# Layer 0 of a four-layer graph network: adj turned by transposing transfers instead of TensorE in six of sixteen batches

## The chip, the core and the metric

The kernel runs on one NeuronCore of a Trainium2 chip, as one launch. The metric is device time in microseconds, the median of three runs. The engines are TensorE (PE, with its weight loads PEld), VectorE (DVE), ScalarE (ACT), GpSimd (POOL) and SyncE (SP). SP and POOL issue the transfers; a transfer issued by SP is on the hardware queue, one issued by POOL on the software queue. Both share the core's 16 DMA engines.

## The reference

Input is `x` of 16 x 1024 x 128 float32 and a 0/1 matrix `adj` of 16 x 1024 x 1024 int32. Four layers follow each other, each adding to `x`. Only layer 0 is touched by the change:

```python
adjT = jnp.transpose(adj.astype(jnp.float32), (0, 2, 1))
w = _masked_row_softmax(adjT)
region = jnp.matmul(w, features)
region = jnp.matmul(region, kernel_1) + bias_1
region = _batch_norm(region, gamma_1, beta_1)
people = jnp.matmul(jnp.transpose(w, (0, 2, 1)), region)
people = jnp.matmul(people, kernel_2) + bias_2
people = _batch_norm(people, gamma_2, beta_2)
```

`features` is relu of the layer norm of `x`. As adj holds 0 and 1, a row of the softmax is the row of adjT over its sum, so two products with adj are needed: one with adjT and one with adj itself. The batch norms take their statistics over all batches; layers 1 to 3 (attention per batch) start when they are known.

## The kernel before, in words

**Rows.** For each of 16 batches, `first_layer` loads the 1024 rows of adj as eight tiles `a` of 128 x 1024, cast to fp8 by the transfer (L372, issued by POOL, 18 places of `a`, so a little over two batches). `load_x` (L366) fetches x.

**Features.** DVE and POOL make the layer norm and split it in two float16 halves in `hv` (`stats`, `aggregate`, `power`, `centre`, `upper`, `lower`; L382 to L401).

**Turning adj.** For the second product adj must lie turned in `at`. In `turn` (L418) TensorE transposes the rows, two fp8 at a time as one float16 word: a step is eight transposes into one PSUM bank, four steps to a batch. `square` (L426) then takes every other byte of the bank by ACT, squares it (0 and 1 stay) and sums each row into `sums`: two squares to a bank, eight to a batch. `share` (L434 to L437, DVE) makes the reciprocals `rc` of the row sums.

**First product.** `product` (L459) is eight steps of eight matmuls, each step into a PSUM bank of its own. `low` (L463, ACT) scales the low half by `rc`, `join` (L467, DVE) adds the halves into `r`; after both the bank is free. `high` (L471, POOL) and `rest` (L474, DVE) make `rv`. `spread` (L352) adds `r` to a gram matrix.

**Second product.** `product2` (L499) is eight steps of eight matmuls with `at`; `low2` (L503, ACT) and `join2` (L506, DVE) empty the bank into `g`, `spread2` (L352) adds to the second gram matrix, and two `turn2` steps (L533) with `save` (L536, ACT) turn the result. `store` (L443) and `store_g` (L542) send `at` and the result to DRAM through SP, except for the last three batches, which stay on the chip.

**Order.** Nothing is scheduled by the hardware. Each action is a `Step` with an engine, a cost in us and the tiles it reads and writes. `Plan` simulates the engines and picks at each moment the ready step of least rank; the rank is the due time of the step's batch (`L0_DUES`, one number per batch and two for the work on the norms) less the length of the work that still follows it. What comes out is an order of instructions for each engine, which the chip then runs as written: an engine waits at the head of its list, even where a later instruction could go. Tiles have fixed numbers of places; PSUM banks (`ps`) have six in layer 0. Layers 1 to 3 have a plan and due times of their own.

Of the kernel before, what the change touches and what calls it, by code (L numbers as in the profile page):

```python
# [9 lines left out]
F16 = mybir.dt.float16  # L10
F8 = mybir.dt.float8e4
# [3 lines left out]
AF = mybir.ActivationFunctionType  # L15
# [4 lines left out]
P = 128  # L20
# [13 lines left out]
LEVEL = 1638.0  # L34
XG_TILES = 6
WEIGHTS_AT = 40.0
L0_DUES, L0_WITHIN = [
    3.2, 51.2, 72.4, 90.5, 112.6, 124.5, 191.4, 204.9, 159.2, 265.6, 223.0, 273.4, 306.2, 325.8, 419.8, 408.3,
    419.5, 419.5,
], 0.1  # L40
DUES, WITHIN = [
    36.4, 58.6, 170.2, 88.0, 111.8, 130.8, 151.3, 175.9, 196.5, 210.6, 240.2, 262.1, 277.1, 318.5, 339.5,
# [21 lines left out]
class Plan:  # L64
# [11 lines left out]
    def room(self, kind):  # L76
        return Room(kind)
# [137 lines left out]
def gnn_stack(ctx: ExitStack, tc: tile.TileContext, x, adj, k1, b1, g1, be1, k2, b2, g2, be2,  # L215
# [45 lines left out]
    with tc.manual_schedule(), ExitStack() as rooms:  # L261
        plan = first_layer(tc, rooms, x, adj, adj_t, gt_rows, qall, ident, ident_h, mhalf, held)
        weights = load_weights(nc, plan, rooms, tc, k1, b1, g1, be1, k2, b2, g2, be2, w1, a1, e0, w3, a3, edge, CB)
        norms(nc, plan, weights, qall, q9, rows9, ident, ones, mhalf, gat1, gat3, edge, shift, kcs, flag, B * N)
        plan.emit(L0_DUES.__getitem__, L0_WITHIN)
        kept = {kind: plan.kept(kind) for kind in held}
# [11 lines left out]
def load_weights(nc, plan, rooms, tc, k1, b1, g1, be1, k2, b2, g2, be2, w1, a1, e0, w3, a3, edge, CB):  # L278
# [7 lines left out]
    def fetch(t, *parts):  # L286
        for n, (dst, src) in enumerate(parts):
            plan.step("sp", 0.1, lambda dst=dst, src=src: nc.sync.dma_start(dst(t), src), (),
                      [(id(t), n) if n else id(t)], 4096, 2, since=WEIGHTS_AT)

# [17 lines left out]
def first_layer(tc, rooms, x, adj, adj_t, gt_rows, qall, ident, ident_h, mhalf, held):  # L308
    nc = tc.nc
    B, N, D = x.shape  # L310
    NB = N // P
# [4 lines left out]
    def places(kind, count, shape, dtype):  # L316
        return [pool.tile(shape, dtype, name=f"{kind}{i}") for i in range(count)]
# [13 lines left out]
        "mv": places("mva", 3, [P, NB, 2], F32),  # L331
        "col": places("cola", 8, [P, NB], F32),
        "ps": [banks.tile([P, 512], F32, name=f"psa{i}") for i in range(6)],
    }
    gram = [banks.tile([P, 512], F32, name=f"gram{i}") for i in range(2)]
    okay = pool.tile([P, B, 2, NB], F32, name="okay")
# [18 lines left out]
    def batch(b):  # L355
        def step(engine, us, run, reads=(), writes=(), moved=0):
            plan.step(engine, us, run, reads, writes, moved, b)

        room = plan.room
        rows = [room("a") for _ in range(NB)]  # L360
# [48 lines left out]
        step("dve", 1.2, lower, [y, (hv, 0)], [(hv, 1)])  # L409

        at, sums, rc = room("at"), room("col"), room("col")
        for w in range(NB // 2):
            ps = room("ps")

            def turn(w=w, ps=ps):
                t = ps.ap.bitcast(F16)
                for j in range(NB):
                    nc.tensor.transpose(t[:, j * P : (j + 1) * P],  # L418
                                        rows[j].ap.bitcast(F16)[:, w * P : (w + 1) * P], ident_h)

            step("pe", 0.47, turn, rows, [ps])
            for t in range(2):
                i = 2 * w + t

                def square(i=i, t=t, ps=ps):
                    nc.scalar.activation(at.ap[:, i, :], ps.ap.bitcast(F8)[:, t::2], AF.Square,  # L426
                                         saturate=False, accum_out=sums.ap[:, i : i + 1])

                step("act", 1.22, square, [ps], [(at, i), (sums, i)])
# [119 lines left out]
    for b in range(B):  # L549
        batch(b)  # L550
# [3 lines left out]
def norms(nc, plan, w, qall, q9, rows9, ident, ones, mhalf, gat1, gat3, edge, shift, kcs, flag, count):  # L554
# [94 lines left out]

    plan.step("dve", 0.8, choose, (), ["masks"], 0, 4, since=WEIGHTS_AT)  # L650
    group[0] = B + 1
# [1010 lines left out]
```

## Time and profile before

| | |
|---|---|
| time, median of 3 runs | 1434.28 us (1432.99 to 1434.79) |
| the profiled execution's own time | 1433.68 us |
| its span in the profile | 1431.8 us, granted clock 0.996 |
| PE, DVE, ACT, POOL busy | 96%, 77%, 56%, 26% |
| layer 0 with its norms, on PE | from 7.4 to 369 us |
| layers 1 to 3 | the rest |

In a row of a group, the columns are line, engine and operation, what is written and read, shapes, how many, then busy time in us with the mean ns of one, then the idle time of the engine just before them and what ended it. Lines are those of the kernel before. In a timeline the columns are start and length in us, engine, line, operation, and how many were merged; matmuls overlap, so what one costs is read from start to start.

### The profile page before, as it was taken

Reading aid. Unit: us, or ns where it says so; the run is one execution under the profiler, and the core shown is the slowest. Engines: PE = TensorE matmul, PEld = TensorE weight load, DVE = VectorE, ACT = ScalarE, POOL = GpSimd, SP = SyncE. Lnnn points to the kernel's source line nnn. Section 1 sums busy time; section 2 is a strip of 40 time slices with the busy share of each in tenths; the row PEclk is TensorE's granted clock in tenths of the full one; section 3 lists DMA queues with packets and bytes.
Section 4 is the critical chain, followed back from the end, with each engine's and each line's share of the span. In section 5 each row is a group of like instructions: output and inputs, shape, how many; then the busy total and the mean of one; then the engine's idle time right before and its main releaser. Section 6 shows DMA issues by size and latency. Waiting matters only on the chain.

```text
span 1431.8 us, 30397 instructions
## 1 busy us (share of the span) xinstructions
PE 1378.6 (96%) x11710; PEld 1264.3 (88%) x11710; DVE 1099.3 (77%) x3148; ACT 795.8 (56%) x2123; POOL 365.7 (26%) x469
## 2 busy tenths in 40 slices
PE   4999999999999999999999999999999999999997
PEld 3889899898899889899999998898988999988797
DVE  4878665554788778788979878789788879787795
ACT  3766776666554554546455545646365644456633
POOL 7788676563211010111111001011011111110010
PEclk9999999999999999999999999999999999999999
DMA  9998987870300021111111211112112012000011
GB/s 156 151 181 166 124 161 148 122 89 2 119 16 16 16 89 46 60 46 60 45 60 45 75 54 54 43 60 101 34 60 72 34 46 75 16 1 1 27 50 47
DMA packets 56347, 99.05 MB, mean 69 GB/s; under 512 B 6296, under 2 KB 45568, under 8 KB 52864
## 3 DMA queue, kind: packets, MB, share of 16 engines
q1 hardware_dynamic: 37472, 79.17, 15.8%
q0 software_dynamic: 18720, 17.83, 14.4%
q8 instruction: 94, 1.54, 0.4%
q14 instruction: 61, 0.50, 0.1%
HBM read 118.37 MB, written 28.95 MB: 103 GB/s over the span
## 4 chain that ended last, share of the span: by engine, by line
PE 71%; DVE 14%; ACT 5%; issue 3%; POOL 3%; DMA 2%; SPq 0%; DVEq 0%; ACTq 0%; POOLq 0%
PE psc L955 35%; PE psa L459 8%; PE psa L499 7%; PE psc L1091 5%; DVE xg L1060 4%; PE gram L352 4%; PE psc L996 3%; PE psc L932 2%; PE psc L1123 2%; PE psa L418 2%; PE psc L881 1%; DVE xg L1112 1%; DVE eu L1109 1%; DVE st L903 1%; ACT y L928 1%
## 5 line engine op out<-in xcount | busy, mean ns | idle before, releaser
L955 PEld LDWEIGHTS psc<-v,xg 128*128 128x128 f32 x4096 | 472.3, 192 | 13.7 <-issue 6.8
L955 PE MATMUL psc<-v,xg 128*128 128x129 f32 x4096 | 482.7, 275 | 1.3 <-DVE xg L1060 1.3
L955 PEld LDWEIGHTS psc<-h,xg 128*128 128x128 f32 x2048 | 238.1, 192 | 20.9 <-DVE xg L1127 12.0
L955 PE MATMUL psc<-h,xg 128*128 128x129 f32 x2048 | 247.5, 276 | 6.1 <-DVE xg L1127 5.2
L914 POOL TENSOR_SCALAR col<-mv 128x8 f32<-128x8 f32 x48 | 28.4, 591 | 878.7 <-DVE mv L909 843.2
L1060 DVE SCALAR_TENSOR_TENSOR xg<-ub,tri,at 128x1024 f32<-128x1024 f32 x176 | 217.3, 1275 | 15.0 <-DMA at<-adj_t 8.8
L1099 ACT ACTIVATE eu<-psc,edge_shift 128x512 f32<-128x512 f32 x192 | 114.3, 595 | 170.4 <-PE psc L1091 170.1
L426 ACT ACTIVATE at<-psa 128x1024 fp8e4<-128x1024 fp8e4 x128 | 131.2, 1033 | 44.7 <-PE psa L418 42.9
L1091 PE MATMUL psc<-gt,gt 128*128 128x512 f32 (+3 forms) x384 | 150.0, 492 | 3.7 <-ACT e L1095 1.8
L1109 DVE SCALAR_TENSOR_TENSOR eu<-e,edge_shift,eu 128x1024 f32<-128x1024 f32 (+7 forms) x128 | 103.8, 811 | 35.6 <-ACT e L1095 35.2
L459 PE MATMUL psa<-hv,a 128*128 128x257 f16 x1024 | 120.8, 278 | 3.3 <-DVE hv L401 3.3
L499 PE MATMUL psa<-rv,at 128*128 128x259 f16 x1024 | 120.0, 275 | 2.6 <-DVE g L506 2.2
L928 ACT ACTIVATE y<-xg,col 128x128 f32<-128x128 f32 x256 | 78.7, 397 | 77.9 <-DVE col L911 74.9
L459 PEld LDWEIGHTS <-a 128*128 128x128 fp8e4 x1024 | 101.5, 99 | 19.1 <-issue 3.5
L499 PEld LDWEIGHTS <-at 128*128 128x128 fp8e4 x1024 | 99.6, 98 | 19.0 <-issue 3.5
L1095 ACT ACTIVATE e<-psc,edge_shift 128x512 f32<-128x512 f32 x192 | 114.3, 595 | 0.0
L973 ACT ACTIVATE y<-psc,col 128x128 f32<-128x128 f32 x256 | 72.0, 393 | 65.0 <-DVE col L967 63.7
L1060 DVE SCALAR_TENSOR_TENSOR xg<-ub,tri,atc 128x1024 f32<-128x1024 f32 x80 | 99.5, 1275 | 1.4 <-DMA ub<-u_rows 0.9
L471 POOL TENSOR_SCALAR rv<-r,cola 128x128 f16<-128x128 f32 x128 | 82.0, 651 | 61.4 <-DVE r L467 61.2
L1147 ACT ACTIVATE y<-psc,col 128x128 f32<-128x128 f32 x256 | 68.9, 419 | 50.2 <-DVE col L1141 49.4
L915 POOL TENSOR_TENSOR col<-col,mhalf 128x8 f32<-128x8 f32 x48 | 93.3, 1945 | 4.0
L935 ACT ACTIVATE gt<-psc 128x512 f32<-128x512 f32 x96 | 54.9, 609 | 52.7 <-PE psc L932 45.5
(209 smaller groups left out, 1963.6 us busy)
## 6 DMA issues: line engine op xcount, KB each, us to landing
a<-in_adj_dram POOLq DMA_DIRECT2D x128, 128.0 KB, 7.4
ub<-u_rows SPq DMA_DIRECT2D x29, 512.0 KB, 3.8
xb<-in_x_dram SPq DMA_DIRECT2D x27, 512.0 KB, 6.9
adj_t<-at SPq DMA_DIRECT2D x13, 1024.0 KB
at<-adj_t SPq DMA_DIRECT2D x8, 1024.0 KB
out_dram<-y SPq DMA_DIRECT2D x16, 512.0 KB
gt_rows<-xg SPq DMA_DIRECT2D x13, 512.0 KB, 5.8
xg<-gt_rows SPq DMA_DIRECT2D x13, 512.0 KB, 5.0
```

What stands on the lines that cost most here:

```text
L426: nc.scalar.activation(at.ap[:, i, :], ps.ap.bitcast(F8)[:, t::2], AF.Square, saturate=False, accum_out=sums.ap[:, i : i + 1])
L459: nc.tensor.matmul(ps.ap[:, : 2 * D + 1], block[:, i % 2 :: 2], hv.ap[:, j, :], start=(j == 0), stop=(j == NB - 1))
L471: nc.gpsimd.tensor_scalar_mul(rv.ap[:, i, 0:D], r.ap[:, i, :D], rc.ap[:, i : i + 1])
L499: nc.tensor.matmul(ps.ap[:, :W2], at.ap[:, i, j * P : (j + 1) * P], rv.ap[:, i, :], start=(i == 0), stop=(i == NB - 1))
L915: nc.gpsimd.tensor_tensor(rs.ap, va.ap, mhalf, ALU.pow)
L928: nc.scalar.activation(y.ap[:, n, :], xs(n), AF.Relu, bias=nm.ap[:, n : n + 1])
L955: nc.tensor.matmul(acc[g].ap[:, k * V1 : (k + 1) * V1], weights[m].ap[:, n * P : (n + 1) * P], values.ap[:, m, :], start=(m == 0 and k == ...
L1060: nc.vector.scalar_tensor_tensor(q[m].ap, ub.ap, ex.ap[:, m, 1:2], at.ap[:, m, :], ALU.max, ALU.mult)
L1091: nc.tensor.matmul(ps.ap[:, : len(c)], ha.ap[:, m * P : (m + 1) * P], ht.ap[:, m * P + c[0] : m * P + c[-1] + 1], start=True, stop=True)
L1095: nc.scalar.activation(e.ap[:, c[0] : c[-1] + 1], ps.ap[:, : len(c)], AF.Exp, bias=shift[:, 0:1], scale=1.0 - SLOPE)
L1099: nc.scalar.activation(eu.ap[:, ROW[m] + c[0] : ROW[m] + c[-1] + 1], ps.ap[:, : len(c)], AF.Exp, bias=shift[:, 1:2], scale=SLOPE)
L1109: nc.vector.scalar_tensor_tensor(t, e.ap[:, :wide], shift[:, 2:3], t, ALU.max, ALU.mult)
```

## The change

In batches 4, 6, 8, 10, 12 and 14 the rows are not turned by TensorE. Instead SP issues, for each of the eight row tiles, a transfer from the tile to the tile `words` with `transpose=True` (on-chip memory to on-chip memory, float16 words, 128 KB). `words` has one place, shared by the six batches. `square_words` takes its bytes from `words` instead of a PSUM bank, and every one of the eight depends on all eight transfers. The other ten batches are turned as before. The due times of layer 0 are other numbers, so the order of the batches and of the steps in layer 0 changes: the batches now follow as 0, 1, 3, 4, 2, 6, 5, 7, 8, 9, 13, 11, 12, 15, 10, 14 on PE. The due times of layers 1 to 3 stay.

```diff
+BY_WIRE = (4, 6, 8, 10, 12, 14)
 L0_DUES, L0_WITHIN = [
-    3.2, 51.2, 72.4, 90.5, 112.6, 124.5, 191.4, 204.9, 159.2, 265.6, 223.0, 273.4, 306.2, 325.8, 419.8, 408.3,
-    419.5, 419.5,
+    -156.8, -24.9, 63.9, 30.7, 37.7, 127.6, 115.7, 136.2, 173.9, 182.5, 327.5, 248.6, 257.8, 236.3, 354.8,
+    266.9, 354.9, 354.9,
 ], 0.1
...
+        "words": places("words", 1, [P, NB // 2, N], F16),
...
         at, sums, rc = room("at"), room("col"), room("col")
-        for w in range(NB // 2):
+        by_wire = b in BY_WIRE
+        if by_wire:
+            words = room("words")
+
+            def turn_row(j):
+                nc.sync.dma_start(words.ap[:, :, j * P : (j + 1) * P], rows[j].ap.bitcast(F16), transpose=True)
+
+            for j in range(NB):
+                step("sp", 1.3, lambda j=j: turn_row(j), [rows[j]], [(words, j)], P * N * 2)
+            for i in range(NB):
+                def square_words(i=i):
+                    nc.scalar.activation(at.ap[:, i, :], words.ap[:, i // 2, :].bitcast(F8)[:, i % 2 :: 2], AF.Square,
+                                         saturate=False, accum_out=sums.ap[:, i : i + 1])
+
+                step("act", 1.0, square_words, [(words, j) for j in range(NB)], [(at, i), (sums, i)])
+        for w in range(0 if by_wire else NB // 2):
             ps = room("ps")
```

## The prediction

> **What bounds the kernel now.** First the page, for the share of each engine and the slices.
>
> ```profile
> PE 1378.6 (96%) x11710; PEld 1264.3 (88%) x11710; DVE 1099.3 (77%) x3148; ACT 795.8 (56%) x2123; POOL 365.7 (26%) x469
> ...
> PE   4999999999999999999999999999999999999997
> ...
> DMA  9998987870300021111111211112112012000011
> ```
>
> TensorE is at nine tenths or more in every slice but the first and the last, and the DMA engines are nearly full in the first nine or ten slices, which are layer 0. The windows tell whether that holds in the stage that changes (columns: PE, PEld, DVE, ACT, POOL busy, granted clock, DMA share, GB/s):
>
> ```profile
> 180.00:216.00 36.00, 36.00 (x354) 32.59 (x353) 23.96 (x101) 25.55 (x60) 27.92 (x38) 1.00 0.90 152
> 216.00:252.00 36.00, 36.00 (x340) 32.52 (x339) 20.43 (x83) 23.54 (x56) 25.13 (x43) 1.00 0.78 146
> ```
>
> PE has no idle time there; ACT is two thirds busy. So what leaves PE in layer 0 shortens the kernel, if nothing comes in its place. PE's timeline gives one batch:
>
> ```profile
> 153.45 1.95 PE L352 MATMUL gram<-g 128*128 128x130 f32 x16
> 155.23 1.04 PE L533 MATMUL psa<-ident,g 128*128 128x128 f32 x8
> 156.11 7.34 PE L459 MATMUL psa<-hv,a 128*128 128x257 f16 x64
> 163.29 1.95 PE L352 MATMUL gram<-r 128*128 128x129 f32 x16
> 165.07 1.95 PE L418 MATMUL psa<-ident_h,a 128*128 128x128 f16 x32
> 166.86 7.53 PE L499 MATMUL psa<-rv,at 128*128 128x259 f16 x64
> ```
>
> Start to start, the 32 transposes of L418 take 1.79 us, a bank of `product` (8 matmuls) 0.90, `product2` the same, a `spread2` step 0.22, the two `turn2` steps 0.88. ACT's timeline gives the squares:
>
> ```profile
> 187.30 1.01 ACT L426 ACTIVATE at<-psa 128x1024 fp8e4<-128x1024 fp8e4 x1
> 188.20 0.20 ACT L426 ACTIVATION_READ_ACCUMULATOR at<-psa 128x1 f32 x1
> 188.29 1.02 ACT L426 ACTIVATE at<-psa 128x1024 fp8e4<-128x1024 fp8e4 x1
> 189.20 0.21 ACT L426 ACTIVATION_READ_ACCUMULATOR at<-psa 128x1 f32 x1
> 189.29 0.69 ACT L503 COPY t<-psa 128x130 f32<-128x130 f32 x2
> ```
>
> Back to back a square with its sum costs 1.00 us, not 1.03 + 0.21. The same view shows them interleaved with the copies of `low2`, under the `product2` of the batch before: now they cost PE nothing.
>
> ```profile
> L426 ACT ACTIVATE at<-psa 128x1024 fp8e4<-128x1024 fp8e4 x128 | 131.2, 1033 | 44.7 <-PE psa L418 42.9 <-DVE rv L474 1.8
> L463 ACT ACTIVATE t<-psa,level,cola 128x129 f32<-128x129 f32 x128 | 54.7, 461 | 42.3 <-PE psa L459 28.5 <-DVE cola L435 8.9 <-DVE r L467 3.9
> L1075 ACT ACTIVATE h<-y 128x1024 f32<-128x1024 f32 x16 | 17.2, 1077 | 32.4 <-DVE y L925 32.4
> ```
>
> The second row is the point of this case. `low` waits for L435, the reciprocal of all eight row sums: until the last square of a batch is done, no bank of that batch's `product` can be emptied, and there are six banks.
>
> **What is removed.** In six batches 192 of the 512 L418 transposes go: 6 x 1.79 = 10.7 us of PE. The built program has 320 left.
>
> **What is added on ACT, and the new wait.** Each `square_words` needs all eight transposed rows, so the eight may run as one block. Where the built order puts them decides. I take, per batch, the PE step whose copy is last on ACT ahead of the block, and count both engines from its end. After the last square comes a fixed tail: 0.15 for the sum, 0.43 to L435, 0.46 for `low`, 0.35 for `join`: 1.4 us until a bank is free. PE meanwhile has what stands before the batch's seventh `product`.
>
> Batch 4: after `product2` of batch 3, ACT has a `low2` (0.27), 8 squares, the tail: 9.7. PE has 5 products (4.5) and 8 `spread2` (1.8): 6.3. PE waits 3.4.
> Batch 6: after `product2` of batch 2, ACT has a `low2`, 2 squares, 2 `save` (1.06), 6 squares, tail: 10.7. PE has 5 `spread2` (1.1), `turn2` (0.9), 2 products (1.8): 3.8. Wait 6.9.
> Batch 8: after `turn2` of batch 7, ACT has the rest of `save` (0.8), 8 squares, tail: 10.2. PE has 6 products: 5.4. Wait 4.8.
> Batch 12: after `product2` of batch 11, ACT has 6 squares, one `low2`, tail: 7.7. PE has 8 `spread2` and 6 products: 7.2. Wait 0.5.
> Batch 10: after `product2` of batch 15, 5 squares, `low2`, 2 `save`, tail: 7.7; PE 8.1. No wait.
> Batch 14: after `turn2` of batch 10, ACT has `save` to 1.6, 5 squares, tail: 8.0; PE 5 products: 4.5. Wait 3.5.
>
> The waits sum to 19.1 us. Queued behind them on PE are the batch's last two products and everything after; on ACT, the `low` copies behind the squares. In the trace of before PE has 0.9 us of idle time between 55 and 350 us (0.24, 0.38 and 0.27 in its timeline), so all of it is new.
>
> The squares now read SBUF, and no row shows that for fp8. The nearest from SBUF of that length is L1075: 1.077 against 1.033, so 0.044 us more for each, in the five batches that wait 5 x 8 x 0.044 = 1.8 us.
>
> **What is added on SP and the DMA engines.** 48 transposing transfers of 128 KB, eight to a batch, each after its row has landed. No row shows such a transfer, so bounds. By bytes: the first rows, 512 KB read each, land 1.25 us apart, so 128 KB takes 0.3 us. By pieces: between 46 and 50 us the hardware queue carried little but the small weight columns:
>
> ```profile
> q0 software_dynamic: 452, 0.41, 110.5%
> q1 hardware_dynamic: 305, 0.00, 9.8%
> ```
>
> 305 packets took 9.8% of 16 engines for 4 us, 21 ns each. The built transfer is cut in tiles of 16 rows by 128 words: 512 runs of 256 bytes on the reading side give 0.7 us over 16 engines, 4,096 runs of 32 bytes on the writing side 5.4. I take 0.7, since this is one on-chip move of a small transfer, and keep 5.4 for the range.
>
> At 0.7 nothing waits. A pair of batches takes PE some 41 us, the DMA engines are busy for about 0.88 of that now, and the free 5 us over eight transfers is 0.6 to 0.8 us each with the new waits counted. `words` has one place: the tightest reuse is batch 14 behind batch 10, with some 11 us of PE work between the last square of one and the first of the other, less 3.8 us (the shortest landing of a row in the trace): 0.9 us each. SP itself has gaps of 10 to 20 us between issues; the stores and x loads queued behind a transpose have a batch of slack. If that cover goes, each 0.1 us beyond 0.8 costs at most 48 x 0.1 = 4.8 us.
>
> A rule of the skill bears on this. The Trainium skill ("DMA: Bandwidth & Descriptors", section "Latency and other measured facts") gives 261 GB/s as the effective rate of a transposing transfer: an estimate of 0.5 us for 128 KB, by which they stay hidden and the sum is unchanged; no row here shows it. Against the change stands "VectorE: DVE Perf Modes", section "Rules for kernel authors": a 128 by 128 transpose belongs on TensorE where PSUM will do as destination. The trace has PSUM at no price for it but the 1.79 us.
>
> **Layers 1 to 3** keep their order instruction for instruction; they start later or earlier as a block.
>
> **The sum.** -10.7 + 19.1 + 1.8 = +10.2 us on the profiled execution's 1433.68, 1443.9; the median of the runs is 0.6 above it: 1444.5.
>
> **The rivals.** *The wait is covered and only the saving is left.* That is one mechanism, the length of a square from SBUF. At 0.8 us the waits are 1.8, 5.3, 3.2, 2.5 and 0: 12.8, and the time 1436.4; at 0.73 they equal the saving; below 0.63 the kernel is faster by over 2.9 us; with all waits gone it is 1423.6. For it speaks only that the source's own step costs give 1.0 for a square from words and 1.22 for one from PSUM, a ratio that would make 0.82 of the measured 1.00. Against it L1075, which is no quicker from SBUF. Chance 0.07 for faster, 0.07 for no change.
>
> *The transfers become the bound.* From 0.8 us each. At 1.3 us the DMA engines owe at most 48 x 0.5 = 24 us, so 1468; if the queues' lead takes it up, only batch 14's 8 x 0.4 = 3 us, 1448. At 5.4 us it is 220 us and 1665. For it: the slices at 9, and 32-byte writes. Chance 0.15.
>
> *The transposes do not leave PE*: excluded by the built order.
>
> **How the numbers follow.** The forecast has 0.71: 1444.5, its own range 1437 to 1455 (squares of 0.8 to 1.1 us with the bank waits following, transfers up to 0.9). The range reaches up to the second rival at 1.3 us: 1437 to 1468. Left out are the first rival below and the dear transfers above, about 0.1 each. About 0.2% or 2.9 us is what a measurement of this kernel tells from no change. Faster 0.07, within 0.07, slower 0.86.
>
> **What would show it.** Right: 320 transposes on PE; new PE idle time before `product` in batches 4, 6, 8 and 14, some 3 to 7 us each, released by `join` behind `low` behind the squares; squares from `words` back to back at 1.0 us; layers 1 to 3 of equal length; words landed before ACT is free. Wrong: squares much under 0.8 us, ACT waiting for a DMA at `square_words` (then the second rival), or PE idle before some other step.

## The result, and the profile after

The changed kernel takes 1457.27 us (median of 5 runs, 1453.07 to 1457.43) against 1434.54 us for the kernel before (5 runs): a ratio of 1.0149 (1.0135 to 1.0162), 22.7 us slower. The forecast was 10.2 us slower, with a range of 1437 to 1468: the direction was right, the time lay inside the range, the size was 12.5 us too small. The profiled execution took 1457.38 us with a span of 1455.6, so it can be set against the 1433.68 and 1431.8 of before. Two of the five executions took 1453 to 1454 us, at a mean granted clock of 0.991 instead of 0.987 to 0.989, so the profile is of one of the longer ones.

First the page of the changed kernel: busy time, then PE and DMA by slices.

```profile
PE 1376.0 (95%) x11518; PEld 1258.8 (86%) x11518; DVE 1104.1 (76%) x3148; ACT 796.8 (55%) x2123; POOL 366.9 (25%) x469
...
PE   4989898999899999999999999999999999999997
...
DMA  9999896987120002100211201111210212000011
```

PE has 192 instructions fewer, as the diff says, and still is busy for only 2.6 us less. The slices that fell to 8 are all in layer 0. The same two windows as before (PE, PEld, DVE, ACT, POOL busy, granted clock, DMA share, GB/s) show what took their place:

```profile
180.00:216.00 36.00, 36.00 (x338) 32.55 (x337) 22.69 (x95) 21.30 (x51) 26.84 (x42) 1.00 1.07 145
216.00:252.00 36.00, 30.40 (x284) 26.95 (x282) 21.82 (x81) 25.15 (x57) 25.08 (x33) 0.91 0.61 129
```

PE now has 5.6 us without work in the second window, and the clock there is 0.91 instead of 1.00. Line numbers of the changed kernel are 17 higher below the change (L459 is now L476) and 2 higher above it (L352 is now L354); `square_words` is L425 and its transfer L419. These are the rows of PE's timeline, from 45 us on, that have over 2 us of idle time before them (in brackets, with what ended it):

```profile
103.46 3.40 PE L476 MATMUL psa<-hv,a 128*128 128x257 f16 x16 [3.84 <-DVE r L484]
128.92 1.96 PE L476 MATMUL psa<-hv,a 128*128 128x257 f16 x16 [2.13 <-DVE r L484]
155.37 3.35 PE L476 MATMUL psa<-hv,a 128*128 128x257 f16 x16 [6.15 <-DVE r L484]
222.22 3.60 PE L476 MATMUL psa<-hv,a 128*128 128x257 f16 x16 [5.05 <-DVE r L484]
372.15 2.52 PE L476 MATMUL psa<-hv,a 128*128 128x257 f16 x16 [3.44 <-DVE r L484]
```

Each is the seventh and eighth `product` of a batch (16 matmuls), kept from its PSUM bank by `join` (L484). The rows at 103, 155, 222 and 372 us are batches 4, 6, 8 and 14. The one at 128.92 us is batch 2, which TensorE still turns. There is a second thing to read in these rows: the length. The same 16 matmuls take 1.96 us after the short wait and 3.35 to 3.60 us after the three longest. The windows of the idle time and of the work right after it give the reason, again with the granted clock as the third number from the right. The last two lines are of batch 14:

```profile
155.37:159.00 3.63, 3.63 (x20) 2.72 (x20) 2.56 (x8) 2.01 (x6) 3.58 (x6) 0.59 0.99 301
217.00:222.22 5.22, 0.18 (x2) 0.00 (x1) 1.15 (x6) 4.66 (x11) 0.00 (x0) 0.76 0.39 146
222.22:227.00 4.78, 4.78 (x25) 3.81 (x25) 3.22 (x11) 2.24 (x6) 4.49 (x8) 0.54 0.42 170
372.15:373.30 1.15, 1.15 (x11) 1.01 (x11) 1.15 (x4) 1.15 (x4) 1.03 (x2) 1.00 0.00 0
373.40:376.70 3.30, 3.30 (x18) 3.04 (x16) 2.53 (x9) 0.87 (x3) 3.30 (x6) 0.50 0.00 0
```

In these windows behind the waits the mean clock is 0.54 and 0.59. Finer windows show it at 0.50 from 103.7 to 107.1 us (batch 4), from 151.5 to 158.3 (batch 6), from 219.8 to 226.5 (batch 8) and from 373.4 to 376.7 (batch 14). At batches 6 and 8 it falls while PE still waits; at batch 14 it falls only 1.2 us after the product has begun. ACT's timeline shows what was done during the wait that ended at 222.22 us:

```profile
219.63 1.04 ACT L425 ACTIVATE at<-words 128x1024 fp8e4<-128x1024 fp8e4 x1
220.58 0.19 ACT L425 ACTIVATION_READ_ACCUMULATOR at<-words 128x1 f32 x1
221.33 2.21 ACT L480 ACTIVATE t<-psa,level,cola 128x129 f32<-128x129 f32 x6 [0.56 <-DVE cola L452]
```

Eight squares from `words` run back to back from 212.35 us on, 1.04 us from start to start; this is the last of them. Behind it stand six `low` copies (L480, merged here in one row), whose products had long been done. The group of these squares says how much ACT waited for the transfers:

```profile
L425 ACT ACTIVATE at<-words 128x1024 fp8e4<-128x1024 fp8e4 x48 | 50.2, 1053 | 1.6 <-DMA words<-a 1.6
```

1.6 us, in all. The list of issues gives the median time from issue to landing:

```profile
words<-a SPq DMA_TRANSPOSE x48, 5.6
```

And this is the hardware queue in the table of queues of the kernel before, with packets, MB and share of 16 engines:

```profile
q1 hardware_dynamic: 37472, 79.17, 15.8%
```

The same row of the changed kernel:

```profile
q1 hardware_dynamic: 63584, 85.47, 19.1%
```

The 26,112 new packets are 544 to a transfer: 512 pieces and some, not 4,096. The queue's time grew from 15.8% of 1431.8 us to 19.1% of 1455.6, that is by 51.8 us, or 1.08 us of all 16 engines for each transfer. (Against the same order without transfers, 15.4% of 1455.3 us in a run below, it is 1.12.)

**Where the time went**, on the two profiled executions. The first matmul of layers 1 to 3 starts at 395.84 us instead of 370.03: 25.8 us later. Layers 1 to 3 take 1059.8 us instead of 1061.8; why they are 2.0 us shorter with the same order is open. Of the 25.8 us, from PE's timelines:

| | us |
|---|---|
| 192 transposes gone | -10.7 |
| waits at the seventh product, batches 4, 6, 8, 12, 14 | +18.9 |
| wait at the seventh product of batch 2 | +2.1 |
| other waits from 45 us on, 0.2 to 1.3 us each, over those of before | +4.6 |
| waits before 45 us | +2.1 |
| slow matmuls from 45 us on, nearly all behind the four long waits (7.0 against 0.3) | +6.7 |
| not placed | +2.1 |

### The profile page after: what moved, and what is told of

Same layout as the page of the kernel before. It is cut to its first block, busy times and chain, and to the rows that moved or that the text cites. A ratio compares the mean times of both kernels' runs of the same rounds, so it can differ in the third digit from the quotient of the medians.

```text
span 1455.6 us, 30113 instructions
## 1 busy us (share of the span) xinstructions
PE 1376.0 (95%) x11518; PEld 1258.8 (86%) x11518; DVE 1104.1 (76%) x3148; ACT 796.8 (55%) x2123; POOL 366.9 (25%) x469
## 3 DMA queue, kind: packets, MB, share of 16 engines
q1 hardware_dynamic: 63584, 85.47, 19.1%
## 4 chain that ended last, share of the span: by engine, by line
PE 68%; DVE 13%; ACT 8%; issue 4%; POOL 4%; DMA 2%; SPq 1%; ACTq 0%; POOLq 0%; DVEq 0%
PE psc L972 36%; PE psa L516 6%; PE psc L1108 6%; PE psa L476 5%; DVE xg L1077 3%; ACT at L425 3%; PE psc L1013 3%; PE gram L354 3%; PE psc L1140 2%; PE psc L949 2%; PE psc L898 2%; DVE xg L1129 1%; DVE st L920 1%; DVE eu L1126 1%; ACT y L945 1%
## 5 line engine op out<-in xcount | busy, mean ns | idle before, releaser
L1077 DVE SCALAR_TENSOR_TENSOR xg<-ub,tri,at 128x1024 f32<-128x1024 f32 x176 | 217.4, 1275 | 10.9 <-DMA at<-adj_t 5.8
L476 PE MATMUL psa<-hv,a 128*128 128x257 f16 x1024 | 127.2, 283 | 26.1 <-DVE r L484 21.8
L476 PEld LDWEIGHTS <-a 128*128 128x128 fp8e4 x1024 | 103.5, 101 | 44.9 <-issue 27.2
L443 ACT ACTIVATE at<-psa 128x1024 fp8e4<-128x1024 fp8e4 x80 | 82.0, 1033 | 31.0 <-PE psa L435 29.7
L920 DVE BATCH_NORM_STATS2 st<-xg 128x6 f32<-128x128 f32 x384 | 82.2, 278 | 0.8
```

Of the source, the lines that this page charges most:

```text
L476: nc.tensor.matmul(ps.ap[:, : 2 * D + 1], block[:, i % 2 :: 2], hv.ap[:, j, :], start=(j == 0), stop=(j == NB - 1))
L920: nc.vector.bn_stats(st.ap[:, n, :], xs(n))
L1077: nc.vector.scalar_tensor_tensor(q[m].ap, ub.ap, ex.ap[:, m, 1:2], at.ap[:, m, :], ALU.max, ALU.mult)
```

## The experiments

Theory 1: the eight squares that run as one block on ACT hold up the `low` copies, so PE waits for a bank, and after such a wait its clock is low; the transfers are hidden. One rival: the transfers cost the time, by what they take of SP or of the DMA engines. The other: the new due times, so the new order, cost the time by themselves. The last is told apart by the four combinations of order and transfers, of which two are the kernels before and after.

**Transfers in the old order**

```diff
 L0_DUES, L0_WITHIN = [
-    -156.8, -24.9, 63.9, 30.7, ...
+    3.2, 51.2, 72.4, 90.5, ...
```

> The six batches go by wire, but layer 0 keeps the due times of before, so the batches stay in the old order. Theory 1 (the block of eight squares on ACT holds the banks of product, and PE runs cold after each such wait): the block is there whatever the due times; along the built order, with the rows' durations, PE waits about 6, 5, 11.5, 2.3, 2.6 and 1.6 us before the seventh product of the six batches, some 29 us in all, less 10.7 us of transposes, plus about 1.5 us of cold clock behind each long wait and 3 us of smaller waits: 1455 to 1470. Rival A (the transfers crowd the DMA engines): about as the changed kernel, 1450 to 1460, with PE or ACT waiting for DMA. Rival B (it is the new due times that cost): the transposes' saving is left, 1424 to 1434.

Measured 1464.25 us, ratio 1.0213 (1.0196 to 1.0230), as theory 1 had it; the rival of the due times had 1424 to 1434. PE's waits are again at the seventh product, 5.92, 4.89 and 11.28 us the longest, and the 16 matmuls behind each take 3.6 us. So the new due times do not make these waits; they make them smaller.

**The new order without transfers**

```diff
-BY_WIRE = (4, 6, 8, 10, 12, 14)
+BY_WIRE = ()
```

> The changed kernel with an empty list of batches by wire: the new due times alone, all sixteen batches turned by TensorE. Theory 1 (the block of squares is the cost): no block of eight squares is left, the squares come two to a bank; along this order they are still close ahead of product in batches 2, 4, 8, 10 and 14, where PE waits 0.7 to 1.4 us at a time, ten times, none long enough for the clock to fall far: 1440 to 1450. Rival B (the new due times cost, not the wire): as the changed kernel or worse by the 10.7 us of transposes, 1457 to 1468.

Measured 1457.79 us, ratio 1.0161 (1.0145 to 1.0176). Theory 1, with 1440 to 1450, missed here, and the range of the rival of the due times, 1457 to 1468, held: the new order is as slow without one transfer as with 48. In its table of waits (us in total, times, longest), DVE's wait for the squares of a batch was 31.2 us before and is

```profile
DVE cola L451 <- ACT at L443: 48.6, 11, 10.7
```

and PE has a wait that the kernel before did not have over 0.5 us:

```profile
PE psa L476 <- ACT at L443: 6.2, 9, 1.0
```

PE has 19.8 us of idle time after 45 us (before: 3.7) in waits of up to 2.5 us; the row above is the largest group, a `product` that wants a bank which a square still reads. The new due times were found for a layer 0 in which the squares of six batches need no bank. So the effects do not add: on the old order the turning by transfer costs 30 us (1464.25 - 1434.54), on the new one nothing (1457.27 against 1457.79).

**The changed kernel without its transfers**

```diff
             def turn_row(j):
-                nc.sync.dma_start(words.ap[:, :, j * P : (j + 1) * P], rows[j].ap.bitcast(F16), transpose=True)
+                pass
```

`words` holds a constant, so the second product of six batches does not see adj, and two tests on the row sums pass always.

> The changed kernel with its order instruction for instruction, but the 48 transposing transfers are not issued: words is filled once with a constant, the squares read that, and the two tests on the row sums pass always, so layer 0 computes with wrong weights; the work of every engine is the same. Theory 1: the transfers were hidden, the block on ACT and the cold clock are still there: 1450 to 1458, PE's waits before the seventh product within 1 us of 3.8, 6.2, 2.1, 5.1 and 3.4. Rival A: the time falls to 1434 or lower, since the transfers were what cost. Rival B: as theory 1.

Measured 1456.04 us, ratio 1.0147 (1.0129 to 1.0165), with PE's waits where they were (3.78, 2.77, 6.14, 5.04 and 3.12 us). In the changed kernel the transfers cost nothing that can be told from the spread: the medians are 1.2 us apart, and the executions of the two overlap.

**The clock kept up during the waits**

```diff
+FILL = {4: 62, 6: 100, 8: 82, 14: 54}
...
+                for _ in range(FILL.get(b, 0) if i == 6 else 0):
+                    nc.tensor.matmul(gram[0][:, 2 * P : 3 * P], ident_h, ident_h, start=False, stop=True,
+                                     skip_group_check=True)
```

> The changed kernel, with matmuls of no use (ident_h by ident_h into an unused part of a gram bank) put on PE just ahead of the seventh product in batches 4, 6, 8 and 14: 62, 100, 82 and 54 of them, 0.056 us each, so 3.5, 5.6, 4.6 and 3.0 us inside waits of 3.8, 6.2, 5.1 and 3.4 us. They add work and take away idle time only. Theory 1 with its cold clock: the two products and the gram steps behind each wait go back to full speed, 1.3 to 1.9 us each, 5 to 7 us in all: about 1451. If the clock has no part in it (the slow matmuls are slow for another reason, DMA traffic into their operands, say): no change, 1457, or up to 2 us more. Rivals A and B: no change.

Measured 1449.89 us (1445.89 to 1451.17), ratio 1.0100 (1.0078 to 1.0122): 7.4 us less than the changed kernel, with 298 matmuls more. PE's timeline at batch 4, filler and then the seventh product:

```profile
99.51 3.62 PE L476 MATMUL gram<-ident_h 128*128 128x128 f16 x62
103.52 1.96 PE L480 MATMUL psa<-hv,a 128*128 128x257 f16 x16 [0.38 <-DVE r L488]
```

The product starts at the same time as in the changed kernel (103.46) and takes 1.96 us instead of 3.40. The slow matmuls after 45 us fall from 7.0 to 1.5 us. The granted clock is 1.00 from 103.5 to 107 us, and so it is behind the other three filled waits. The clock behind the waits is shown, with its price.

**Half the block**

```diff
-                    nc.scalar.activation(at.ap[:, i, :], words.ap[:, i // 2, :].bitcast(F8)[:, i % 2 :: 2], AF.Square,
+                    nc.scalar.activation(at.ap[:, i, : N // 2], words.ap[:, i // 2, : N // 2].bitcast(F8)[:, i % 2 :: 2], AF.Square,
...
```

The two tests on the row sums pass always here too.

> The changed kernel with its transfers, order and due times, but each of the 48 squares from words does half a row (512 elements), so at is only half new and the row sums are of half rows in six batches. If the block of squares on ACT is what PE waits for, 8 squares cost about 4.4 us instead of 8.4 and the waits of 3.84, 6.15, 5.05, 0.46 and 3.44 us fall to about 0.2, 2.5, 1.4, 0 and 1.2: -13.6, and with them most of the slow matmuls behind, -4: 1437 to 1443. Rival, that something else holds PE there (transfers, order): 1452 to 1457.

Measured 1442.35 us (7 runs, 1437.73 to 1448.43), ratio 1.0051 (1.0033 to 1.0069). A square takes 0.614 us from start to start instead of 1.04, so a block is 3.4 us shorter, and 14.9 us of the 22.7 are gone. The waits at the seventh product of the six batches sum to 8.9 us instead of 18.9. That it is the block on ACT that PE waits for is shown by its size.

One wait hardly moved: batch 4's went from 3.84 to 2.95 us. DVE's timeline tells why:

```profile
99.79 2.14 DVE L396 TENSOR_SCALAR ya<-xb,mva,cola 128x128 f32<-128x128 f32 x8 [2.12 <-POOL cola L392]
101.85 0.16 DVE L451 TENSOR_SCALAR cola<-cola 128x8 f32<-128x8 f32 x1
```

The squares end at 99.2 us, but `share` (L451) stands on DVE behind `centre` (L396) of another batch, which waited 2.12 us for `power` on POOL. In the changed kernel `centre` ended 0.8 us before the squares did (101.28 against 102.06), so this second wait was hidden by the first.

**Transfers added to the kernel before**, 48 in groups of eight from a tile of ones to a tile that nobody reads, so that only their use of SP and of the DMA engines counts. First behind the stores of `at` of batches 3, 5, 7, 9, 11 and 12, then behind the x loads of batches 7, 9, 11, 12, 13 and 14:

```diff
+            for j in range(NB if b in (3, 5, 7, 9, 11, 12) else 0):
+                nc.sync.dma_start(kinds["words"][0][:, :, j * P : (j + 1) * P], kinds["still"][0], transpose=True)
```

> The kernel before, with PE, ACT and POOL in the same order, and besides 48 transposing transfers of 128 KB from a constant tile to a tile that nobody reads, eight at a time on SP behind the store of at of batches 3, 5, 7, 9, 11 and 12. Nothing waits for them but SP's own list. Theory 1: DMA engines have room for them; 1434 to 1438. Rival A: row and x loads land late, PE waits for DMA in layer 0, 1445 to 1460.

> The kernel before with the same 48 idle transfers as in the run that had them behind the stores of at, but now eight at a time behind an x load that no other x load follows on SP at once (batches 7, 9, 11, 12, 13, 14). If the 14 us of that run came from one x load that stood behind eight transfers on SP's list (its 10.9 us wait of PE at batch 4), not from the DMA engines: 1433 to 1437. If the transfers cost by crowding the DMA engines: 1440 or more.

Measured 1448.71 us, ratio 1.0104 (1.0087 to 1.0121), and 1456.22 us, ratio 1.0162 (1.0146 to 1.0177): theory 1 missed both, and the ranges for transfers that crowd the DMA engines, 1445 to 1460 and 1440 or more, held. In the first, one group is enough. This is SP's own timeline:

```profile
91.05 13.79 SPq L448 DMA_TRANSPOSE words<-still  x8
104.94 0.53 SPq L547 DMA_DIRECT2D gt_rows<-xg  x1
105.57 1.35 SPq L369 DMA_DIRECT2D xb<-in_x_dram  x2
```

And this the wait that it made, in the table of waits:

```profile
DVE sta L385 <- DMA xb<-in_x_dram: 11.0, 1, 11.0
```

SP is held for 1.27 to 2.48 us by each transfer, 1.72 on average, against some 0.5 us for a plain one. The x load behind them goes out at 105.57 us instead of 94.45. DVE waits 11.0 us for it, and PE 10.9 us at 121.51. The list is not all of it, though. In the trace's records of single packets the group's 4,096 pieces of 256 bytes move from 95.4 to 113.4 us, and the 1 KB packets of x, which stand behind them on the hardware queue, only after that. The last packet of this load ends at 118.3 us, and at 98.6 in the kernel before: 19.7 us late, of which SP's list makes 11.1.

In the second run SP's timeline has this group, ahead of the load that PE's longest wait comes from:

```profile
74.55 20.66 SPq L371 DMA_TRANSPOSE words<-still  x8
```

Its pieces move until 104.6 us. The chain of work up to PE's wait has

```profile
96.64 20.85 DMA xb<-in_x_dram
```

So this load went out only 2.2 us later than in the kernel before, and landed 20.9 us after its issue. PE waits 8.27, 3.19 and 3.24 us, with 8.3 us of slow matmuls behind them. So the transfers are not free as such: what stands behind them on SP's list, and behind their pieces on the hardware queue, comes late. Whether the pieces alone take so long, or the row loads of adj beside them slow them down, was not told apart.

**A better order.** If the planner's cost model was the fault, measured costs should mend it: squares 1.0 and 1.05 us, 1.5 us of SP for a transfer, landing 2.9 us at 400 KB to the us, and due times searched anew against these.

```diff
+MEASURED = {"square": 1.0, "square_words": 1.05, "low": 0.41, "join": 0.27, ...
+        for s in plan.steps:
+            s.us = 1.5 if s.engine == "sp" and s.moved == P * N * 2 else MEASURED.get(s.run.__name__, s.us)
+        plan.RATE, plan.LAND = 400e3, 2.9
         plan.emit(L0_DUES.__getitem__, L0_WITHIN)
```

> The six batches by wire as in the changed kernel, but the plan of layer 0 is made with step costs as measured (a square 1.0 us, a transfer 1.5 us on SP, loads at the pace of the trace, copies at their pitch), and due times found for these. In the order that comes out the squares of a batch by wire stand singly between the copies of the batch before, ahead of its products. Theory 1: the waits of over 1 us before the seventh product go, the clock stays up, the transposes' 10.7 us are left less some small waits: 1424 to 1430. Rival A or a theory in which ACT or the transfers are too slow for six batches in any order: 1440 or more.

> The order and due times of the run with the planner's costs as measured (1458.81), with the 48 transposing transfers left out: words holds a constant, so the second product of six batches does not see adj. If the transfers' lateness (ACT waiting for words 16.9 us at most, DVE for x 12.1 at most) is all that this order loses, PE's waits go: 1458.8 less some 30 us, 1424 to 1432. Rival, that the order itself or the block of eight squares on ACT costs it: 1445 to 1459 without the transfers too.

With the transfers 1458.81 us, ratio 1.0178 (1.0164 to 1.0191), a miss by 29 us. Without them 1435.42 us, ratio 1.0001 (0.9992 to 1.0010). The two differ in the transfers alone, so these cost 23.4 us in this order. The waits for DMA in layer 0, from the table of waits of the run with transfers:

```profile
ACT at L431 <- DMA words<-a: 16.9, 4, 7.7
DVE sta L390 <- DMA xb<-in_x_dram: 12.1, 5, 5.4
```

In the run without them one is left:

```profile
DVE sta L391 <- DMA xb<-in_x_dram: 3.2, 3, 2.1
```

This order has no block waits. That it therefore leaves the transfers no slack is argued from the two runs, not tried by itself. And without them it only equals the kernel before, though PE has 10.7 us less to do: 12.5 us of waits after 45 us (3.7 before) and 3.4 us more ahead of that take the saving. The 1424 to 1432 us expected without transfers was a miss too, by 3 us at the near end.

**Fewer transfers, and none, in orders searched in the same way**

```diff
-BY_WIRE = (4, 6, 8, 10, 12, 14)
+BY_WIRE = (14, 15)
```

> Only batches 14 and 15 by transposing transfers (sixteen, issued late in layer 0, where adj's row loads thin out), the planner's costs as measured, due times found anew. 2 x 1.79 = 3.6 us of PE go, and the order gives no wait over 0.5 us if a transfer takes SP 1.5 us: 1428 to 1432. If the transfers take SP 3 us each beside what row loads are left, the stores and the PSUM banks behind them are late: 10 to 14 us more, 1440 to 1446.

> No batch by transfer; the planner's costs as measured and due times found anew by the same search. The order's own effect: if the search finds orders as good as that of the kernel before, 1431 to 1435; if orders that look equal on paper are as dear on the chip as the one with the changed kernel's due times and no transfer was (1457.8), 1440 to 1458.

Measured 1441.06 us, ratio 1.0047 (1.0035 to 1.0060), and 1443.79 us, ratio 1.0066 (1.0053 to 1.0079). Two batches turned late gain 2.7 us on none, near the 2 x 1.79 = 3.6 us of PE; the orders differ as well, so this is no clean price. Both times lie in the range that was given for the worse case; SP is held for 1.2 to 3.8 us by a transfer, 1.6 in the median. The search by itself lost 9 us on the order of before: on the chip PE waits 10.5 to 11.0 us after 45 us instead of 3.7. No version that was run beats the kernel before.

## Why the prediction was right in its direction and wrong in its size

**What is removed.** 192 transposes, as forecast.

**The new wait.** The forecast had 3.4, 6.9, 4.8, 0.5, 0 and 3.5 us for batches 4, 6, 8, 12, 10 and 14. Measured: 3.84, 6.15, 5.05, 0.46, 0 and 3.44. The cause is shown by halving the block. The forecast's sum was 20.9, of which 1.8 was for squares that take 0.044 us longer from SBUF (measured: 1053 against 1033 ns, so 0.020); the measured 18.9 holds both. By the forecast's own counts 35 of these squares stand ahead of the waits, not 40, so that term should have been 1.5.

**Where it failed: the sum** took a wait at its length, and took waits in the six batches alone. The first missing term is *the clock behind a wait, 6.7 us*; the filler gave back 7.4. The trace of before had it in one place already. This is PE's timeline of before, at the product that follows a wait at the start:

```profile
23.39 10.06 PE L459 MATMUL psa<-hv,a 128*128 128x257 f16 x64 [3.31 <-DVE hv L401]
```

And the same timeline at the start of layer 1, after waits of 1.33 and 0.97 us with little work between:

```profile
370.50 3.61 PE L881 MATMUL psc<-kcs,xg 128*128 128x128 f32 x16
...
374.84 2.00 PE L881 MATMUL psc<-kcs,xg 128*128 128x128 f32 x16
```

10.06 us instead of 7.34 for 64 products, 3.61 instead of 2.00 for 16 matmuls: 2.7 and 1.6 us lost. For the second the profile has a granted clock of 0.57 from 370 to 374 us; for the first it has 1.00, so that the clock was the reason there is not shown. Four waits at 1.6 us would have made the forecast 1451. The Trainium skill ("TensorE: Matmul & The Clock Gate", "Part 1: The HAM clock gate") has it as a rule: after an idle window of about 3.4 us the clock is halved until about 3.4 us of work have passed. An estimate from that page is 1.7 us for each of four waits, 6.8 in all; the profile has 7.0. The threshold is not sharp in these runs, though: with the new order alone 1.49 us were lost after a wait of 2.50 us, and after the 2.13 us of batch 2 nothing.

The second missing term is *the waits of the new order outside the six blocks, 2.1 + 4.6 + 2.1 us*. The forecast counted only the squares from `words`. That the order of the other ten batches changes was known, but no wait was worked out for it. PE idle before some other step was among the forecast's own signs of being wrong. The new order without any transfer, 23 us slower, shows that an order is a cost of its own; what makes each of the small waits was not tried.

The third is *what could not be placed, 2.1 us*. Together 17.6 us were left out; the waits of the sum were 2.0 too high, and layers 1 to 3 gave 2.0. With 0.1 us less outside the span that is the 13.5 us between the forecast for the profiled execution, 1443.9, and its 1457.38.

**The rivals.** *The wait is covered*: it needed squares under 0.8 us; they take 1.04. *The transfers become the bound*: not in the changed kernel, where leaving them out changes nothing (1.0147 against 1.0149), though their price is 1.08 us rather than 0.7. (The forecast had 512 pieces of 21 ns; the trace's records of single packets have 28 ns for a piece of 256 bytes, 0.90 us for a transfer, and the rest of the growth lies in other packets.) The point given for it, 0.8 us of all engines, did not decide. In the order without block waits the transfers do cost, 23.4 us, as this rival had it. (The page before shows the DMA engines at seven to nine tenths in the first nine slices and near nothing in the tenth.) That the waits themselves gave the DMA engines their time in the changed kernel fits both runs, but was not tried by itself.

**The cover on SP.** The forecast said that the stores and x loads queued behind a transpose have a batch of slack. In the changed order they do (DVE waited for x once, 5.1 us, and PE's only wait of some length for features is 0.55 us, at 251 us). In the order of before one group of eight makes the next x load go out 11 us late and land 20 us late, and stops PE for 10.9 us.

**The rule against the change.** "VectorE: DVE Perf Modes", "Rules for kernel authors", leaves a 128 by 128 transpose to TensorE where PSUM will do as destination. These runs agree: a batch costs TensorE 1.79 us, and by transfer it costs, by the growth of the queue's time, 8 x 1.08 = 8.6 us of all 16 DMA engines and at least 8 x 1.2 us of SP. The rate of 261 GB/s in "DMA: Bandwidth & Descriptors" is not reached: 131,072 bytes in 1.08 us are 121 GB/s.

## What to carry to other kernels

Price a wait on TensorE with what follows it: each of the four waits of 3.4 us or more cost another 1.4 to 2.1 us of slow matmuls here, and the trace before the change has such a loss, 1.6 us, at the start of layer 1. When work leaves the busiest engine, look at the step that stays behind on another: here ACT's squares stayed, and a dependence of all on all made them one block in front of the copies that free PSUM. And when an order is made anew, count its waits in every part that it touches, since two orders without any transfer differed by 9 us on the chip (1443.79 against 1434.67).

## What the runs showed of the hardware that was not expected

- A transposing transfer of 128 KB holds SP for 1.2 us at least, 1.5 in the median and 7.9 at most in the changed kernel, and 14.8 once in the second run with added transfers, where a plain one of 512 KB takes some 0.5. What SP waits for is not in the trace. An x load issued behind eight of them landed some 20 us late.
- It makes 544 packets and takes 1.08 us of all 16 DMA engines, by the growth of the queue's time; in that figure is what the transfers and the other loads cost each other.
- TensorE's clock fell to 0.50 at each of four waits of 3.4 to 6.2 us, for 3.3 to 3.4 us at batches 4 and 14 and for 6.7 to 6.8 at 6 and 8, part of it inside the wait. A filler of small matmuls, which nothing reads, gave back 7.4 us.
- A square with its sum costs 1.04 us for 1024 elements and 0.614 for 512; by these two, 0.19 us of it would not depend on the length.
